# A graph attention layer on one core: the products of the segment sums dealt out among the pick products

## The chip, the cores and the metric

The kernel runs on one core of one Trainium2 chip. The metric is the time of one execution in microseconds (us) on the device. The time before is the median of three runs.

## What is computed

The layer has 6250 nodes of 64 values and 206250 edges, which come sorted by their destination. For each edge the scores of four heads are made of the source's key, the destination's query and the edge's own values; the score weighs the source's value, and the weighed values are summed by destination. Then comes a layer norm over the node.

```python
Qh = (x @ Wq.T + bq).reshape(n, H, D)          # n = 6250, H = 4, D = 16
Kh = (x @ Wk.T + bk).reshape(n, H, D)
Vh = (x @ Wv.T + bv).reshape(n, H, D)
Ee = (edge_attr @ We.T + be).reshape(-1, H, D)  # 206250 edges
score = (Kh[src] * Qh[dst] * (1.0 / np.sqrt(D)) * Ee).sum(-1)
score = jnp.exp(jnp.clip(score, -5.0, 5.0))
msg = Vh[src] * score[..., None]
wV = jax.ops.segment_sum(msg, dst, num_segments=n)
x = _layernorm(x + wV.reshape(n, H * D), axis=-1)
```

## The kernel before, in words

**Tiles, groups, steps.** The edges are cut into 1612 tiles of 128. Eight tiles are a group (202 groups, numbered g), and one turn of the main loop (L866 to L963) works on one group. Two groups are a step (numbered s; the last eight groups are steps of their own): the sums by destination are made once for a step. So the odd turn 2s+1 finishes a step's messages, and the even turn 2s+2 sums them.

**What each engine does in turn g, in the order of its own queue.** The order is written out by hand; the loop's text is the order of every engine's queue.

- TensorE (PE): `edges(g+3)` (2 fp32 products into `ee`), in some turns `picked_kv`, then `picks` (21 products of 128x512 in bf16 into one of two PSUM buffers `pick`), `turn(g+1)` (4 transposes of `term` into `qe`), `queries(g+2)` (2 products into `qq`), and in even turns `sums` (16 products of 128x192 in bf16 into `room`).
- VectorE (DVE): `products` (`prod`, `score`), `hots` (the one-hot rows `hot` that the next turn's picks read), `message` (`qe`), `take` twice, in odd turns `onehot_edges` (`of`, L723) and `add` (L804 and twice L810), then `terms(g+2)` (L707, which reads `qq` and `eb`) and parts of the layer norm.
- ScalarE (ACT): the exponential, `biased` (`eb`, out of `ee`), the one-hot rows for the queries (`to`), and `keep` twice (`msg`).
- GpSimd (POOL): indirect DMAs that gather keys and values by source (`kv`, L259), four steps ahead. SyncE (SP) issues the other loads, edges (`et`) and destination keys (`kb`) among them once in two turns.

**The picks.** For some tiles the keys and values are not gathered but picked by products with one-hot rows. `pieces(g)` gives a turn seven blocks, `by_two` deals them in pairs (2, 2, 2, 1), and each block is three products: the last of an even turn's four lots has three products, the others six. This goes on from turn 6 to turn 191.

**The sums.** `sums(s)` (L781) multiplies the step's one-hot columns `of` with the messages split into three bf16 parts, and adds over the 16 tiles in PSUM (`room`). Its first product needs three things of DVE: `of` of the step (made in turn 2s+1), the third parts of its messages (the second `take` of turns 2s and 2s+1), and that `add` of the step before has read `room`. That `add` stands in turn 2s+1 too, behind the second `take` and right ahead of `terms`. The messages' tiles of the first group are older.

**The gathers.** The list `where` collects marks, the PE product that was last issued at a place; the gathers of a turn are dealt evenly over the marks, and the first of each lot waits for its mark (`gather`, `behind`).

Of the kernel before, what the change touches and what calls it, by code (L numbers as in the profile page):

```python
# [21 lines left out]
G = 8  # L22
# [33 lines left out]
def tiles_in(s):  # L56
    return sum(tiles_of(g) for g in groups_of(s))


def groups_of(s):  # L60
    return range(STEPS[s][0], STEPS[s][0] + STEPS[s][1])
# [65 lines left out]
def tile_gnn(ctx: ExitStack, tc: tile.TileContext, x, x_blocks, by_rows, xT, wT, bias, beT, weT, eT, src, src_rows, dst,  # L127
# [159 lines left out]
    with tc.tile_pool(name="nodes", bufs=1) as nodes, \  # L287
# [27 lines left out]
        for i in range(NB // CB):  # L315
            s = slice(i * CB * P, (i + 1) * CB * P)
# [279 lines left out]
    with tc.If(rv == 0) as branch:  # L596

        with tc.tile_pool(name="work", bufs=2) as work, \
# [32 lines left out]
            def pieces(g):  # L631

                some, k, end = [], max(first_unit(g), 0), min(first_unit(g + 1), UNITS * LAST)
                while k < end:
                    some.append((k, min(end, k + MOST, (k // UNITS + 1) * UNITS)))
                    k = some[-1][1]
                return some
# [10 lines left out]
            def by_two(todo):  # L648

                blocks = [(k, w, w + 1 == end) for k, end in todo for w in range(k, end)]  # L650
                return [blocks[i:i + 2] for i in range(0, len(blocks), 2)]

            def picks(todo):

                for k, w, last in todo:
                    hot = HOT.pop(k) if last else HOT[k]
                    m, u = w // UNITS, w % UNITS
                    for part in range(3):
                        product(px[m % 2], parts[:, u, part].rearrange("p t c -> p (t c)"),
                                         hot[:, w - k, :], start=u == 0 and part == 0,  # L660
                                         stop=u == UNITS - 1 and part == 2)
# [20 lines left out]
            def product(*aps, **kw):  # L682
                mark.append(nc.tensor.matmul(*aps, **kw))  # L683
# [93 lines left out]
            def pa_of(s):  # L777

                return {NS - 3: px[0][:, :3 * C], NS - 2: px[1][:, :C], NS - 1: ee[:, 0, :C]}.get(s, pa)

            def sums(s):  # L781
                n = tiles_in(s)
                for j in range(n):
                    product(pa_of(s), (OF if s >= WHOLE else OH)[s][:, j, :],
                            MSG[s][:, j].rearrange("p i c -> p (i c)") if s < WHOLE else MSG[s][:, j, :],
                            start=j == 0, stop=j == n - 1,
                                     skip_group_check=True)
# [64 lines left out]
            ends = {groups_of(s)[-1]: s for s in range(NS)}  # L852
# [13 lines left out]
            for g in range(NG + 1):  # L866
                now, before = g < NG, g > 0
                todo, ahead = pieces(g), pieces(g + 1)
# [15 lines left out]
                parted = now and step_of[g] < WHOLE  # L884
# [27 lines left out]
                    picked_kv(READY.index(g - 2))  # L912
                    place_kv(READY.index(g - 2))
                where.append(mark[-1])
                for some in by_two(todo):
                    picks(some)
                    where.append(mark[-1])
                if g + 1 < NG:
                    turn(g + 1)
# [1 line left out]
                    queries(g + 2)  # L921
                where.append(mark[-1])
                if g - 1 in ends and now:
                    sums(ends[g - 1])
                if g + 4 < NG:
                    onehot_rows_rest(g + 4)
                if parted:
# [5 lines left out]
                for h in ([g] if g < NG - 3 else []) + ([g + 1] if NG - 4 <= g < NG - 1 else []):  # L933
                    if h not in ends:
                        continue
                    s = ends[h]
# [14 lines left out]
                if done:  # L951
# [8 lines left out]
                    for _ in range(3):  # L960
                        if normed < scaled:
                            norm(normed)
                            normed += 1  # L963
            sums(NS - 1)
            spreads(B - 2)
            assert normed == B - 2
# [9 lines left out]
    with branch.Else():  # L976

        sums = [dram.tile([NR, C], F32, name=f"sums{i}") for i in range(TABLES)]
# [108 lines left out]
        with tc.tile_pool(name="last", bufs=1) as last:  # L1087
            B = BIG + 1

            acc = last.tile([P, B, C], F32, name="gacc")  # L1090
            nc.sync.dma_start(acc, x_blocks)
            for i, s in enumerate(sums):
                part = last.tile([P, B, C], F32, name="part", bufs=2)
                (nc.sync, nc.scalar)[i % 2].dma_start(
                    part, s[:P * B, :].rearrange("(b p) c -> p b c", p=P))
                nc.vector.tensor_add(acc, acc, part)
            layer_norm(nc, last, acc, P, B)
            nc.sync.dma_start(out, acc)
# [43 lines left out]
```

## Time and profile before

| | |
|---|---|
| time, median of 3 runs | 2096.95 us (2089.41 to 2100.56) |
| the profiled execution's own time | 2094.31 us |
| its span, first to last instruction | 2092.5 us |
| mean granted TensorE clock | 0.889 of full |
| PE busy | 1697.4 us (81%), 7771 products |
| DVE busy | 1512.8 us (72%) |
| POOL busy | 1352.3 us (65%) |
| ACT busy | 899.7 us (43%) |
| DMA | 229.84 MB, mean 110 GB/s |

The rows of the profile's views name a line of the kernel, an engine, the operation and what it writes and reads (`room<-msg,of` writes the tile `room`). In a timeline a row has the start in us from the span's start, the duration in us, and behind the count, in brackets, the idle time of the engine before it and who ended it; "issue" is idle time for which the profile shows no one that was waited for. In a group's row stand the busy time in us and the mean duration of one in ns, then the idle time before its instructions. Durations of products overlap: the distance between two starts is what one costs.

### The profile page before, as it was taken

What the parts mean: (1) busy time and instruction counts of PE and PEld (TensorE: products, weight loads), DVE (VectorE), ACT (ScalarE), POOL (GpSimd) and SP (SyncE); (2) the same over time, 40 slices, a digit from 0 to 9 for tenths busy, and PEclk for the clock granted to TensorE, in tenths of its full rate; (3) what the DMA queues carried; (4) which work ended last, traced back from release to release, by engine and by line L of the source; (5) the groups of instructions that cost most, each with busy time, mean ns of one, the idle gap of its engine ahead of it and who ended that gap; (6) DMA issues with size and microseconds to landing.
All of it is one profiled execution on the core that took longest, in us unless ns stands there. A gap on an engine that the chain in (4) does not pass through costs nothing.

```text
span 2092.5 us, 24524 instructions
## 1 busy us (share of the span) xinstructions
PE 1697.4 (81%) x7771; PEld 843.7 (40%) x7771; DVE 1512.8 (72%) x2631; ACT 899.7 (43%) x1477; POOL 1352.3 (65%) x1414
## 2 busy tenths in 40 slices
PE   6538888888888888888888888888888898898874
PEld 6313444343444443444444344444343343444432
DVE  5347777777777677777777777767876776777876
ACT  3434444444444345444444444434444443444453
POOL 6666666666666666666666666666666666666643
PEclk9868999999899999998899899898998988988985
DMA  6733434343433443333334344343333433434431
GB/s 177 215 98 105 120 112 110 100 117 92 118 99 105 118 110 98 112 108 112 102 107 116 93 118 112 92 118 104 104 114 104 113 101 109 118 91 117 114 91 30
DMA packets 114977, 229.84 MB, mean 110 GB/s; under 512 B 55955, under 2 KB 56703, under 8 KB 114725
## 3 DMA queue, kind: packets, MB, share of 16 engines
q1 hardware_dynamic: 69474, 136.35, 21.6%
q0 software_dynamic: 44928, 90.79, 16.9%
q10 hardware_dynamic: 436, 1.04, 0.2%
q8 instruction: 63, 1.03, 0.2%
q14 instruction: 76, 0.62, 0.1%
HBM read 220.25 MB, written 7.82 MB: 109 GB/s over the span
## 4 chain that ended last, share of the span: by engine, by line
PE 60%; DVE 14%; issue 13%; ACT 5%; another core or an unknown queue 3%; DMA 3%; SPq 0%; DVEq 0%; POOL 0%; ACTq 0%; POOLq 0%
PE pick L683 40%; PE ee L683 8%; PE room L683 6%; PE qe L712 3%; PE qq L683 2%; DVE hot L643 2%; DMA qw<-q_tab 2%; DVE prod L731 2%; DVE score L734 2%; DVE qe L769 1%; ACT to L242 1%; DVE term L707 1%; ACT eb L694 1%; DVE msg L769 1%
## 5 line engine op out<-in xcount | busy, mean ns | idle before, releaser
L259 POOL DMA_INDIRECT kv<-kv_tab,src_i x1364 | 1312.8, 962 | 692.9 <-issue 320.9
L683 PE MATMUL pick<-hot,parts 128*128 128x512 bf16 x3900 | 976.9, 402 | 76.1 <-issue 68.4
L683 PEld LDWEIGHTS <-parts 128*128 128x128 bf16 x3900 | 396.1, 103 | 684.2 <-issue 331.6
L740 ACT ACTIVATE score<-score 128x32 f32<-128x32 f32 x202 | 46.3, 229 | 984.5 <-DVE score L736 654.9
L643 DVE TENSOR_TENSOR hot<-from,still 128x1024 bf16<-128x1024 bf16 (+4 forms) x379 | 394.2, 1043 | 0.0
L707 DVE TENSOR_TENSOR term<-eb,qq 128x512 f32<-128x512 f32 x202 | 137.7, 682 | 291.3 <-PE pick L683 147.5
L683 PE MATMUL ee<-et,we_sb 128*128 128x512 f32 x404 | 262.0, 728 | 53.3 <-issue 24.8
L683 PE MATMUL room<-msg,of 128*128 128x192 bf16 x1592 | 188.9, 266 | 122.0 <-issue 97.2
L764 ACT ACTIVATE msg<-qe 128x512 bf16<-128x512 f32 x400 | 237.2, 593 | 16.8 <-issue 6.6
L248 ACT ACTIVATE to<-to,one_p 126x1024 bf16<-126x1024 bf16 x198 | 226.4, 1143 | 0.0
L242 ACT ACTIVATE to<-kb,minus_row 126x1024 bf16<-126x1024 bf16 x198 | 224.6, 1135 | 0.0
L769 DVE TENSOR_TENSOR qe<-qe,msg 128x512 f32<-128x512 f32 x200 | 139.7, 699 | 117.4 <-ACT msg L764 81.8
L683 PEld LDWEIGHTS <-of 128*128 128x128 bf16 x1600 | 141.5, 105 | 162.7 <-issue 137.8
L769 DVE TENSOR_TENSOR msg<-qe,msg 128x512 bf16<-128x512 f32 x200 | 137.4, 687 | 86.8 <-issue 40.6
L694 ACT ACTIVATE eb<-ee,be_col 128x512 f32<-128x512 f32 x202 | 136.4, 675 | 109.6 <-PE pick L683 47.7
L712 PE MATMUL qe<-ident,term 128*128 128x128 f32 x806 | 131.5, 287 | 52.8 <-DVE term L707 44.6
L712 PEld LDWEIGHTS qe<-ident,term 128*128 128x128 f32 x806 | 104.7, 148 | 107.5 <-DVE term L707 57.1
L731 DVE TENSOR_TENSOR prod<-kv,qe 128x512 f32<-128x512 f32 x202 | 137.4, 680 | 12.1 <-remote 6.6
L734 DVE TENSOR_REDUCE score<-prod 128x32 f32<-128x512 f32 x202 | 138.3, 685 | 7.0
L752 DVE TENSOR_TENSOR qe<-kv,score 128x512 f32<-128x512 f32 x200 | 138.9, 695 | 4.3 <-ACT score L740 2.7
L723 DVE TENSOR_TENSOR of<-still,key 128x2048 bf16<-128x2048 bf16 (+2 forms) x105 | 123.0, 1173 | 0.2
L683 PEld LDWEIGHTS ee<-et,we_sb 128*128 128x128 f32 x404 | 71.8, 217 | 95.4 <-issue 54.7
(138 smaller groups left out, 848.5 us busy)
## 6 DMA issues: line engine op xcount, KB each, us to landing
et<-in_eT SPq DMA_DIRECT2D x100, 512.0 KB
kb<-key_tab SPq DMA_DIRECT2D x101, 504.0 KB
kv<-kv_tab,src_i POOLq DMA_INDIRECT x1364
srcs<-in_src_rows SPq DMA_DIRECT2D x52, 256.0 KB
qw<-q_tab SPq DMA_DIRECT2D x202, 15.8 KB
kv_tab<-kv_sb SPq DMA_DIRECT2D x4, 640.0 KB
q_tab<-q SPq DMA_DIRECT2D x5, 480.0 KB
y<-in_x_blocks SPq DMA_DIRECT2D x2, 512.0 KB
```

Of the source, the lines that this page charges most:

```text
L242: nc.scalar.activation(TO[g][:, :n, :], KB.pop(g)[:, :n * P].rearrange("p (j e) -> p j e", j=n), AF.Square, bias=minus_row3[:3 * W])
L248: nc.scalar.activation(TO[g][:, :n, :], TO[g][:, :n, :], AF.Relu, bias=one_p[:3 * W], scale=-1.0)
L259: return nc.gpsimd.indirect_dma_start(out=kv_of(g)[:, j, :], out_offset=None, in_=kv_tab[:, :], in_offset=bass.IndirectOffsetOnAxis(ap=src ...
L643: nc.vector.tensor_tensor(HOT[k][:, :hi - lo].rearrange("p b (a c) -> p b a c", c=2), pairs(FROM[m])[:, None].to_broadcast(shape), block2[ ...
L683: mark.append(nc.tensor.matmul(*aps, **kw))
L694: nc.scalar.activation(EB[g][:, :n], ee[:, :n], AF.Identity, bias=be_col)
L707: nc.vector.tensor_mul(TERM[g][:, :n], EB.pop(g)[:, :n], qq[:, :n])
L712: nc.tensor.transpose(qe[g % 2][:, 2 * u:2 * u + 2, :].rearrange("p j c -> p (j c)"), TERM[g][:, u, :], ident)
L731: nc.vector.tensor_mul(prod[:, :n, :], kv_of(g)[:, :n, :C], qe[g % 2][:, :n, :])
L734: nc.vector.tensor_reduce(score, prod[:, :n, :].rearrange("p g (h d) -> p g h d", h=H), axis=AX.X, op=OP.add)
L764: nc.scalar.activation(part, left, AF.Copy)
L769: nc.vector.tensor_sub(left if i == 0 else part_of(g, 2)[1], left, part)
```

## The change

`sums` gets a range of tiles. In an even turn with picks, four of its products are issued behind the second, the third and the fourth lot of picks, twelve in all. The last four stay where all sixteen stood, behind the transposes and the queries. Where a turn has no picks (the first and the last ones), and for the last two steps, nothing is moved. The marks in `where` are taken behind the dealt-out products. No instruction is added and none is taken away.

```diff
-            def sums(s):
+            def sums(s, lo=0, hi=2 * G):
                 n = tiles_in(s)
-                for j in range(n):
+                for j in range(lo, min(hi, n)):
                     product(pa_of(s), (OF if s >= WHOLE else OH)[s][:, j, :],
                             MSG[s][:, j].rearrange("p i c -> p (i c)") if s < WHOLE else MSG[s][:, j, :],
                             start=j == 0, stop=j == n - 1,
...
-                for some in by_two(todo):
+                summed = 0
+                for i, some in enumerate(by_two(todo)):
                     picks(some)
+                    if i and parted and g - 1 in ends:
+                        sums(ends[g - 1], summed, summed + 4)
+                        summed += 4
                     where.append(mark[-1])
                 if g + 1 < NG:
                     turn(g + 1)
@@
                 where.append(mark[-1])
                 if g - 1 in ends and now:
-                    sums(ends[g - 1])
+                    sums(ends[g - 1], summed)
```

## The prediction

> **What bounds the kernel now.** I read the page first: its busy line, its chain, and its costliest groups.
>
> ```profile
> PE 1697.4 (81%) x7771; PEld 843.7 (40%) x7771; DVE 1512.8 (72%) x2631; ACT 899.7 (43%) x1477; POOL 1352.3 (65%) x1414
> ...
> PE 60%; DVE 14%; issue 13%; ACT 5%; another core or an unknown queue 3%; DMA 3%; SPq 0%; DVEq 0%; POOL 0%; ACTq 0%; POOLq 0%
> ...
> L683 PE MATMUL pick<-hot,parts 128*128 128x512 bf16 x3900 | 976.9, 402 | 76.1 <-issue 68.4
> ...
> L707 DVE TENSOR_TENSOR term<-eb,qq 128x512 f32<-128x512 f32 x202 | 137.7, 682 | 291.3 <-PE pick L683 147.5
> ...
> L683 PE MATMUL room<-msg,of 128*128 128x192 bf16 x1592 | 188.9, 266 | 122.0 <-issue 97.2
> ```
>
> PE carries 60% of the chain and DVE 14%: PE is the bound, and DVE has a little slack, which shows in its idle time ahead of `term`, 291.3 us in 202 (1.44 us each), most of it behind PE. The row to look at is the last one. The sums are a fifth of PE's products but have the most idle time of all, 122.0 us, and 97.2 us of it has no releaser. The timeline of PE shows what that is; the first seven rows are an even turn and what follows it, the others a later even turn and its odd one.
>
> ```profile
> 604.54 0.92 PE L683 MATMUL room<-msg,of 128*128 128x192 bf16 x9
> 605.91 0.32 PE L683 MATMUL room<-msg,of 128*128 128x192 bf16 x2 [0.45 <-issue]
> 607.33 0.33 PE L683 MATMUL room<-msg,of 128*128 128x192 bf16 x2 [1.09 <-issue]
> ...
> 609.48 0.32 PE L683 MATMUL room<-msg,of 128*128 128x192 bf16 x1 [0.46 <-issue]
> 610.19 1.87 PE L683 MATMUL ee<-et,we_sb 128*128 128x512 f32 x2 [0.39 <-issue]
> 611.85 5.17 PE L683 MATMUL pick<-hot,parts 128*128 128x512 bf16 x21
> 616.85 0.60 PE L712 MATMUL qe<-ident,term 128*128 128x128 f32 x4
> ...
> 645.35 1.49 PE L683 MATMUL room<-msg,of 128*128 128x192 bf16 x16
> ...
> 653.81 0.59 PE L683 MATMUL pick<-hot,parts 128*128 128x512 bf16 x2 [1.02 <-issue]
> 655.24 0.38 PE L683 MATMUL pick<-hot,parts 128*128 128x512 bf16 x1 [0.84 <-issue]
> 655.95 0.38 PE L683 MATMUL pick<-hot,parts 128*128 128x512 bf16 x1 [0.34 <-issue]
> 656.67 0.38 PE L683 MATMUL pick<-hot,parts 128*128 128x512 bf16 x1 [0.33 <-issue]
> 656.88 0.60 PE L712 MATMUL qe<-ident,term 128*128 128x128 f32 x4
> ```
>
> Undisturbed, a run of sixteen starts its last product 1.25 us after its first (1.49 less the 0.24 of one product): 0.083 us each. In a slow stretch PE gets one product in about 0.7 us (605.91 to 607.33 is two, 655.24 to 655.95 one), whether it is a sum or a pick. So the run of sixteen is often slow, but where it isn't, the picks behind it are: the stretch comes once in two turns and hits what stands there. From the first sum to the next transposes the first pair of turns took 616.85 - 604.54 = 12.31 us, the second 656.88 - 645.35 = 11.53 us.
>
> **The change part by part.** The count of PE's instructions stays, and no buffer changes. There are 92 even turns with picks between 175 and 1994 us, of which the terms below are counted (one more is in the start).
>
> (a) *Order on PE.* Twelve sums of 0.083 us, 1.0 us, now run ahead of the transposes and the queries, and 1.0 us less behind them. A turn's work is the same: 0.
>
> The next rows are PE's in turns 8, 28 and 188, and DVE's second `add` row (`below`) in each, which ends last of what the first sum needs.
>
> ```profile
> 176.86 4.70 PE L683 MATMUL pick<-hot,parts 128*128 128x512 bf16 x21
> ...
> 377.72 4.70 PE L683 MATMUL pick<-hot,parts 128*128 128x512 bf16 x21
> 383.43 0.66 PE L712 MATMUL qe<-ident,term 128*128 128x128 f32 x4 [1.01 <-DVE term L707]
> ...
> 1980.36 4.70 PE L683 MATMUL pick<-hot,parts 128*128 128x512 bf16 x21
> ```
> ```profile
> 180.16 0.28 DVE L810 SCALAR_TENSOR_TENSOR acc<-room,below,acc 128x64 f32<-128x64 f32 x1
> ...
> 382.50 0.28 DVE L810 SCALAR_TENSOR_TENSOR acc<-room,below,acc 128x64 f32<-128x64 f32 x1
> ...
> 1983.78 0.28 DVE L810 SCALAR_TENSOR_TENSOR y<-room,below,y 128x64 f32<-128x64 f32 x1
> ```
>
> (b) *The new place to wait.* The first sum needs DVE's `add` of the turn before. It stood behind 21 picks, 4 transposes and 2 queries; now it stands behind 12 picks. Behind it in PE's queue are 9 picks, the transposes and the queries, and for these DVE's `term`, and the picks' `hot` buffers. What a pick costs is in the row at 377.72 us: 4.70 us for 21, less 0.38 for the last, over 20: 0.216.
>
> In turn 28 twelve picks are done at 377.72 + 2.59 = 380.31 us and the `add` at 382.78: PE would stand 2.47 us. It stands 1.01 there now, at the transposes. Read in this way over all 92 turns, 22 have the `add` late; the first is turn 8 (179.45 against 180.44, 0.99 us) and the last turn 188 (1982.95 against 1984.06, 1.11 us). They come to 19.6 us, of which about 2.8 us are waits that stand at the transposes already: 17 us. In the other 70 the `add` is done before the twelfth pick, and the wait costs nothing.
>
> (c) *DVE later.* The queries of an even turn end 1.0 us later, and DVE's `term` waits for them; with it everything that DVE does up to the next `add` can come 1.0 us later while PE's twelfth pick does not. If all of it came through, 36 turns would be late, by 46 us, less 3. If nothing did (DVE behind anyway, or held by ACT), 17 us stand. The row of `term` has about half its idle time behind picks and the rest elsewhere, so I take half: 30 us.
>
> (d) *Waits that coincide.* In 16 of the 22 late turns the run of sums is slow as well (its last start over 1.5 us after its first). What supplies PE can go on while PE waits for DVE, so part of these waits, 12.5 us of the 19.6, may only take the place of a slow stretch. The bounds are 0 and 12.5; I take half, -6: 24 us are left.
>
> (e) *The slow stretch meets other instructions.* In a slot of 0.7 us a sum does 0.083 us of work and a pick 0.216, so a stretch on picks loses 0.133 us less of each slot, 19%. If all 97.2 us moved from sums to picks, that gives 18 us; if it stayed on sums, 0; if the stretch went away, 12.31 - 11.53 = 0.78 us for each of the 50 slow runs of the 92, 39 us. Four sums still stand behind the queries and four right ahead of the transposes, where the stretch begins now. I take half of the middle case: -9.
>
> ```profile
> L731 DVE TENSOR_TENSOR prod<-kv,qe 128x512 f32<-128x512 f32 x202 | 137.4, 680 | 12.1 <-remote 6.6 <-issue 3.6 <-DMA kv<-kv_tab,src_i 0.2
> ```
> ```profile
> SPq L203 <- PE pick L683: 608.6, 36, 25.8
> ```
> ```profile
> PE pick L683 <- DVE x L665: 20.4, 16, 2.0
> ```
>
> (f) *Things that ride along.* The gathers behind the third to last mark are released 0.3 to 1.0 us later. POOL runs four steps ahead, and `prod` waited 0.2 us for gathered `kv` in the whole span; cost 0, and if that cover went, up to the 1.0 us of a turn. SP's load of `et` waits for PE's first products of an even turn, ahead of everything moved, and in part for picks (36 times), which come at most 0.67 us later; it loads six groups ahead: 0. Where an even turn ends a batch of picks, its last pick comes 0.67 us later and DVE's next step with it; PE waits for that step now 20.4 us in all, in 16 turns. Cost between 0 and 26 batches by 0.67, 17 us; 0, since that step of DVE stands behind a whole turn's other work.
>
> *Sum:* 30 - 6 - 9 = +15 us. On the profiled execution's 2094.31 us (span 2092.5) that is 2109; on the median of the runs, 2.6 us above it, 2112. I forecast **2110 us**.
>
> **The clock.** The next rows follow turn 28: PE's timeline, and busy times by stretch with the mean granted clock as the third number from the right.
>
> ```profile
> 389.51 0.37 PE L683 MATMUL pick<-bkv_p,ones_b 3*128 3x512 bf16 x1 [2.04 <-DVE x L665]
> 389.81 1.16 PE L683 MATMUL pick<-w,x 128*128 128x128 f32 x8
> 390.80 6.38 PE L683 MATMUL pick<-hot,parts 128*128 128x512 bf16 x21
> ```
> ```profile
> 383.40:388.00 4.60, 3.54 (x24) 2.18 (x25) 4.40 (x8) 2.36 (x5) 3.38 (x5) 1.00 0.33 86
> ...
> 390.80:397.00 6.20, 6.20 (x23) 2.53 (x21) 4.17 (x7) 2.41 (x5) 3.00 (x4) 0.72 0.13 36
> ```
>
> A wait can also cost clock. In turn 29 PE waited 2.04 us for DVE, and the picks behind it ran partly at half clock. The 21 picks took 6.38 us instead of 4.70, 1.68 us more, at a mean granted clock of 0.72, while the wait of 1.01 us at 383.43 left the clock at 1.00. The Trainium skill, page "TensorE: Matmul & The Clock Gate", section "Why this matters for your kernels", asks for no gaps over about 3 us between bursts of products; by that rule none of the new waits, 2.47 us at most, would cost clock. The rows differ: 2.04 us with work around it that was thin was enough.
>
> **The rivals.**
>
> *Forecast, the wait decides (0.45).* Terms as above. For it: the `add` is the last thing in DVE's odd turn, and 22 waits can be read off. Against it: 70 turns have it early, by up to 5 us.
>
> *The run of sixteen was what made the stretch (0.24, faster).* Sums ask for instructions at more than twice the rate of picks (0.083 against 0.216 us). If the supply only fails when a dense row of short instructions stands behind the transposes, dealing them out ends it at this place, from the point on where the four that are left no longer run it dry. The price is (e)'s end, -39 us, and with (b) to (d), +24, the sum is -15: 2079 us; if the waits fall into slow stretches as well, 2060. For it: the slow rows at 605.91 begin behind the ninth sum of such a row. Against it: in the second pair the same stretch hits plain picks.
>
> *It comes out even (0.26).* The waits lie in slow stretches (all of (d)) and the stretch moves on to picks (all of (e)'s middle): 30 - 12.5 - 18 = 0, 2094 to 2097 us.
>
> *The waits cost clock too (0.05, slower).* If each of the 22 waits took 1.68 us, 37 us on top: 2146. Against it: only one of them is over 2 us as the trace stands, and five with the 1.0 us of (c).
>
> **How the numbers follow.** About 0.5%, 10.5 us, is what can be told from no change here. The forecast's own bounds are (b) without (c) and with all of (d) and (e), 17 - 12 - 18 = -13, to 43 us without (d) and (e). So slower holds 0.46, most of the forecast's share and the clock's; within 0.5% holds 0.29, the even case and a part of the forecast's; faster 0.25. The range goes from 2070, below the faster rival's 2079, to 2140, the forecast's upper bound; what it leaves out is the faster rival's far end and the clock.
>
> **What would show it.** (b): behind the twelfth pick, sums that wait for DVE's `add` (L810), in 20 to 36 turns, 20 to 45 us in all, where the group of the sums shows next to none in the loop now; the wait of the transposes for `term` in even turns smaller. (c): more idle time of DVE ahead of `term` in even turns. (e): idle time without a releaser ahead of the sums clearly below 97.2 us, and that of the picks (68.4) and of `ee` above what they have. If the sums' falls and the picks' doesn't rise, the faster rival holds. If the sums wait for DVE in under ten turns, (b) is wrong. If the granted clock falls below 0.87, the last rival holds.

## The result, and the profile after

The changed kernel takes 2093.43 us (median of 20 runs, 2089.87 to 2099.18), the kernel before beside it 2094.67 us (20 runs). The ratio is 0.9994, 95% interval 0.9985 to 1.0003: no change. On another chip it was 1.0000 (0.9991 to 1.0009). The forecast was 2110 us.

The rows of the changed kernel's page that answer to those of before (groups: busy us, mean ns of one, idle time before them, what ended it):

```profile
PE 1685.2 (81%) x7771; PEld 842.9 (40%) x7771; DVE 1514.9 (72%) x2631; ACT 899.1 (43%) x1477; POOL 1354.2 (65%) x1414
...
PE 57%; DVE 18%; issue 14%; ACT 5%; another core or an unknown queue 3%; DMA 2%; POOL 1%; DVEq 0%; SPq 0%; ACTq 0%; POOLq 0%
...
L259 POOL DMA_INDIRECT kv<-kv_tab,src_i x1364 | 1314.6, 964 | 688.6 <-issue 328.8
L683 PE MATMUL pick<-hot,parts 128*128 128x512 bf16 x3900 | 978.6, 397 | 37.6 <-issue 35.1
...
L707 DVE TENSOR_TENSOR term<-eb,qq 128x512 f32<-128x512 f32 x202 | 138.0, 683 | 352.1 <-PE room L683 122.3
L683 PE MATMUL room<-msg,of 128*128 128x192 bf16 x1592 | 223.9, 262 | 108.3 <-issue 69.5
```

The sums' idle time without a releaser fell from 97.2 to 69.5 us and the picks' from 68.4 to 35.1. But PE's idle time as a whole is 2092.0 - 1685.2 = 406.8 us, where it was 2092.5 - 1697.4 = 395.1: what left these two rows went elsewhere. The view of PE's waits says where. Its columns are us in all, times, and the longest; first the kernel before, then the changed one, both from turn 8 to turn 191, so that the start and the end of the program stay out.

```profile
PE room L683 <- issue: 97.2, 108, 2.6
PE pick L683 <- issue: 89.1, 147, 2.0
PE ee L683 <- issue: 24.3, 31, 1.9
...
PE qe L712 <- DVE term L707: 10.7, 6, 4.2
PE qq L683 <- issue: 8.8, 7, 1.8
PE qe L712 <- issue: 6.0, 10, 1.1
```
```profile
PE room L683 <- issue: 69.5, 82, 2.6
PE qe L712 <- issue: 60.4, 64, 2.7
PE pick L683 <- issue: 53.0, 99, 2.0
...
PE ee L683 <- issue: 12.9, 17, 1.4
PE qq L683 <- issue: 11.6, 14, 2.4
...
PE qe L712 <- DVE term L707: 6.0, 5, 2.4
PE room L683 <- DVE y L810: 5.7, 7, 1.7
PE room L683 <- DVE room L804: 5.3, 4, 1.7
```

The five rows "issue" come to 97.2 + 89.1 + 24.3 + 8.8 + 6.0 = 225.4 us before and 69.5 + 60.4 + 53.0 + 12.9 + 11.6 = 207.4 after. That is about the same: two kernels below that have no waits of this kind and take the same time, `behind_picks` and `add_early_before`, have 205.6 and 229.5 us in these rows. What changed is its place. It has moved on in the queue to the transposes, 6.0 to 60.4 us, which now follow the first twelve sums directly. The transposes' wait for `term` shrank by 10.7 - 6.0 = 4.7 us, and the sums got waits on DVE that they did not have. Turn 28 in PE's timeline shows such a wait; it stands where the prediction put it:

```profile
374.68 2.75 PE L683 MATMUL pick<-hot,parts 128*128 128x512 bf16 x12
378.81 0.49 PE L683 MATMUL room<-msg,of 128*128 128x192 bf16 x4 [1.37 <-DVE acc L810]
379.13 1.46 PE L683 MATMUL pick<-hot,parts 128*128 128x512 bf16 x6
...
381.74 0.60 PE L712 MATMUL qe<-ident,term 128*128 128x128 f32 x4
```

A wait is read here as the time from the start of the pick ahead of the first sum to the start of that sum, less the 0.216 us of a pick. Over the loop 25 turns have one of over 0.1 us, 23.8 us in all, 1.82 us the longest. Counted from the first `ee` product of a turn to that of the next (turns 8 to 187), even turns became longer, 10.47 to 11.31 us, and odd turns shorter, 9.57 to 8.76; a pair stays at 20.04 and 20.07 us.

### The profile page after: what moved, and what is told of

It reads as the page before. It is cut to its first block, busy times and chain, and to the rows that moved or that the text cites. A ratio compares the mean times of both kernels' runs of the same rounds, so it can differ in the third digit from the quotient of the medians.

```text
span 2092.0 us, 24524 instructions
## 1 busy us (share of the span) xinstructions
PE 1685.2 (81%) x7771; PEld 842.9 (40%) x7771; DVE 1514.9 (72%) x2631; ACT 899.1 (43%) x1477; POOL 1354.2 (65%) x1414
## 4 chain that ended last, share of the span: by engine, by line
PE 57%; DVE 18%; issue 14%; ACT 5%; another core or an unknown queue 3%; DMA 2%; POOL 1%; DVEq 0%; SPq 0%; ACTq 0%; POOLq 0%
PE pick L683 36%; PE ee L683 8%; PE room L683 6%; PE qe L712 3%; DVE hot L643 3%; PE qq L683 2%; DVE score L734 2%; DVE prod L731 2%; DVE qe L769 2%; DVE of L723 2%; ACT to L242 1%; DVE msg L769 1%; DVE qe L752 1%; ACT msg L764 1%
## 5 line engine op out<-in xcount | busy, mean ns | idle before, releaser
L259 POOL DMA_INDIRECT kv<-kv_tab,src_i x1364 | 1314.6, 964 | 688.6 <-issue 328.8
L683 PE MATMUL pick<-hot,parts 128*128 128x512 bf16 x3900 | 978.6, 397 | 37.6 <-issue 35.1
L683 PEld LDWEIGHTS <-parts 128*128 128x128 bf16 x3900 | 395.1, 103 | 574.9 <-issue 248.6
L707 DVE TENSOR_TENSOR term<-eb,qq 128x512 f32<-128x512 f32 x202 | 138.0, 683 | 352.1 <-PE room L683 122.3
L683 PE MATMUL room<-msg,of 128*128 128x192 bf16 x1592 | 223.9, 262 | 108.3 <-issue 69.5
L683 PEld LDWEIGHTS <-of 128*128 128x128 bf16 x1600 | 146.3, 103 | 216.1 <-issue 128.9
L712 PE MATMUL qe<-ident,term 128*128 128x128 f32 x806 | 144.4, 295 | 105.9 <-issue 73.5
L769 DVE TENSOR_TENSOR msg<-qe,msg 128x512 bf16<-128x512 f32 x200 | 137.4, 687 | 91.0 <-ACT msg L764 42.0
L769 DVE TENSOR_TENSOR qe<-qe,msg 128x512 f32<-128x512 f32 x200 | 139.7, 698 | 52.1 <-ACT msg L764 37.3
```

What stands on the lines that cost most here:

```text
L259: return nc.gpsimd.indirect_dma_start(out=kv_of(g)[:, j, :], out_offset=None, in_=kv_tab[:, :], in_offset=bass.IndirectOffsetOnAxis(ap=src ...
L712: nc.tensor.transpose(qe[g % 2][:, 2 * u:2 * u + 2, :].rearrange("p j c -> p (j c)"), TERM[g][:, u, :], ident)
L769: nc.vector.tensor_sub(left if i == 0 else part_of(g, 2)[1], left, part)
```

## The experiments

Two theories. **B**: the waits cost their 24 us, and the slow stretch gave about 24 us back; two terms that happen to cancel. **C**: PE doesn't hold the loop; something else does, and PE's waits, whatever ends them, take slack that is there anyway. (**A**, between them: a wait is absorbed by the slow stretch of its own pair of turns.)

One plain fact is needed to read the numbers. The runs fell on chips of two kinds: on the first the kernel before takes 2095 to 2121 us, on the second 1796 to 1797 us. Every run in the table stands beside runs of the kernel before on its own chip, and its ratio is to these.

| kernel | us | before there | ratio, 95% interval |
|---|---|---|---|
| sums_first | 2101.43 | 2094.74 | 1.0032 (1.0017 to 1.0047) |
| behind_picks | 2094.84 | 2094.74 | 1.0002 (0.9990 to 1.0014) |
| add_early_after | 2093.27 | 2094.74 | 0.9993 (0.9978 to 1.0007) |
| add_early_before | 2095.74 | 2094.74 | 0.9995 (0.9980 to 1.0009) |
| half_sums | 2088.16 | 2095.96 | 0.9958 (0.9943 to 0.9972) |
| two_parts | 2085.35 | 2095.96 | 0.9956 (0.9939 to 0.9973) |
| no_loads | 2093.75 | 2095.96 | 0.9993 (0.9980 to 1.0006) |
| no_gathers | 1727.90 | 2095.96 | 0.8244 (0.8213 to 0.8275) |
| no_marks | 1797.24 | 1796.96 | 1.0002 (0.9992 to 1.0012) |
| half_gathers (the kernel before again) | 1797.50 | 1796.96 | 1.0007 (0.9996 to 1.0017) |
| no_gathers_after | 1673.25 | 1796.96 | 0.9316 (0.9300 to 0.9331) |
| no_gathers_sums_first | 1681.39 | 1796.96 | 0.9367 (0.9351 to 0.9383) |
| changed_again | 2118.67 | 2119.44 | 1.0000 (0.9991 to 1.0009) |
| half_gathers_true | 1740.13 | 2119.44 | 0.8211 (0.8192 to 0.8231) |
| plain_loads | 1739.47 | 2119.44 | 0.8208 (0.8191 to 0.8226) |
| no_gathers_again | 1731.41 | 2119.44 | 0.8170 (0.8151 to 0.8189) |
| no_marks_again | 1797.08 | 1795.64 | 1.0008 (0.9998 to 1.0018) |
| changed_no_marks | 2402.53 | 2121.16 | 1.1331 (1.1316 to 1.1347) |

### Other places for the sums: many waits, little time

`sums_first` puts all sixteen sums ahead of the picks of an even turn, where their waits on DVE are the longest that can be had; `behind_picks` puts the run of sixteen behind the last lot of picks.

```diff
+                early_sums = todo and parted and g - 1 in ends
+                if early_sums:
+                    sums(ends[g - 1])
                 for some in by_two(todo):
                     picks(some)
...
-                if g - 1 in ends and now:
+                if g - 1 in ends and now and not early_sums:
                     sums(ends[g - 1])
```

> All sixteen sums stand ahead of the picks of the even turn. In the trace of before DVE's add ends 1.4 us behind the first pick's start on the mean of 92 even turns, after it in 75 of them, 144 us in all (253 us if DVE comes 1.33 us later as well). If the waits and the slow stretch are two terms that cancelled (B): at least 100 us slower than before, 5%. If waits are absorbed by the slow stretch of the same pair of turns (A): much less than the wait that the trace shows, under half of it, 20 to 70 us. If the loop is not bound by PE at all (C): same as before.

> All sixteen sums stand undealt behind the 21 picks and ahead of the transposes of the even turn. DVE's add is late there in 1 of 92 turns, under 1 us in all, so it has next to none of the wait and none of the dealing. B: slow stretches as before, time within 0.3% of before. The run of sixteen as the cause: still a run, still slow, same as before. A: same as before.

The sums of `sums_first` in the groups with their releasers:

```profile
L683 PE MATMUL room<-msg,of 128*128 128x192 bf16 x1592 | 187.1, 282 | 135.7 <-DVE y L810 63.9 <-DVE room L804 40.9 <-DVE acc L810 15.0
```

63.9 + 40.9 + 15.0 = 119.8 us of waits on the `add`, 101.2 of them between turns 8 and 191, where the kernel before has none; and the time went up by 6.7 us. At this price, 6.7 / 101.2 = 0.07 us for a us of wait (0.04 to 0.10 by the interval), the changed kernel's 23.8 us would cost 1.6 us. That is C's (or A's) answer; B needs the full price. A has a part in it: the rows "issue" of these five products fell from 225.4 to 164.7 us over these turns, well below the 205.6 of `behind_picks`, so some 61 us of the waits took the place of the slow stretch. `behind_picks` neither deals nor waits, and comes out the same too.

### The add made earlier

In the changed kernel the `add` moves ahead of the batch's `picked` in every turn, so that the sums find it done; the same edit in the order of before is the control.

```diff
-                if g > groups_of(ONES - 1)[-1]:
-                    for s in done:
-                        add(s)
+                for s in done:
+                    add(s)
...
-                if g <= groups_of(ONES - 1)[-1]:
-                    for s in done:
-                        add(s)
```

> The changed kernel, with DVE's add moved up in its odd turn to ahead of onehot_edges and the second take, so that the first sum waits for the second take, 0.95 us earlier. The 25 waits of 23.8 us in the trace after become about 12 of 6 us. B: 15 to 18 us faster than the changed kernel, 0.8%. A or C: within 0.3% of it.

> The kernel before with the same early add, as the control: the wait behind the queries was never there, so all theories say within 0.3% of before, unless DVE now waits for PE's sums.

From turn 8 to turn 191 the sums of `add_early_after` don't wait for the `add` at all (idle times of over 0.15 us), where the changed kernel has 5.7, 5.3 and 1.4 us (`y`, L804, `acc`) in twelve waits; 7.6 us on `of` came up. The waits of the change are mostly gone, and the time did not follow: 0.9993, against 0.9994 with them.

### Taking work away

`half_sums` and `two_parts` take products out of PE, `no_loads` the repeated loads out of SP's queue, `no_gathers` the gathers out of POOL.

```diff
-                for j in range(n):
+                few = s < WHOLE and s > 2
+                for j in range(0, n, 2 if few else 1):
...
-                            start=j == 0, stop=j == n - 1,
+                            start=j == 0, stop=j == n - (2 if few else 1),
```
```diff
-                    for part in range(3):
+                    for part in range(0, 3, 2):
```
```diff
-        et = loads.tile([P, LG * G // 2, P], F32, name="et")
-        nc.sync.dma_start(et[:, :hi - lo, :], eT[:, lo:hi, :])
+        if q < 4:
+            kept_et.append(loads.tile([P, LG * G // 2, P], F32, name="et"))
+            nc.sync.dma_start(kept_et[q][:, :hi - lo, :], eT[:, lo:hi, :])
+        et = kept_et[q % 4]
```
```diff
         (g, js), after = lot
+        if 20 <= g < NG - 12:
+            return
         for j in js:
```

(In `no_loads` the load of `kb` is kept in the same way, for its first four tiles.)

> The kernel before, with every second product of the sums left out (776 of 1612; the sums then miss half of the edges). PE bound by its work: 776 by 0.083 us, 64 us less at most. PE bound by the number of its instructions (the supply, 10% of its instructions gone): 100 to 200 us less. PE not the bound of the loop: within 0.5% of before.

> The kernel before, with the middle one of the three products of each pick block left out (1300 of 3900; the picked keys and values lose bits). By PE's work: 1300 by 0.216 us, 281 us less. By the number of instructions, 17% of PE's: 200 to 300 us less. PE not the bound: within 1% of before. What the time falls by less than 281 us is what others hold.

> The kernel before without the loads of et and kb from turn 2 on, so that it works on the edges and keys of the first turns again and again. If the slow stretch of PE is tied to these 1 MB bursts: idle time of PE without a releaser under 60 us instead of some 220 us. If PE is the bound: 200 to 400 us faster. If the bound is elsewhere (DVE with ACT, or POOL): the stretch goes and the time hardly moves, under 3%.

> The kernel before without the gathers of groups 20 to 189, which then use old keys and values. POOL issues a gather every 1.25 us, 13.7 in a pair of turns, 17.1 us of 20.0. If POOL, or the traffic of its gathers, holds the loop: 10% faster or more. If not: within 1%, or as much faster as the slow stretch shrinks.

The picks in the groups of `two_parts`, and then the chain and the picks of `no_gathers`:

```profile
L683 PE MATMUL pick<-hot,parts 128*128 128x512 bf16 x2600 | 719.5, 426 | 113.5 <-issue 109.4
```
```profile
DVE 62%; ACT 20%; PE 9%; issue 5%; another core or an unknown queue 2%; DMA 1%; POOL 1%; POOLq 0%; DVEq 0%; SPq 0%; ACTq 0%
...
L685 PE MATMUL pick<-hot,parts 128*128 128x512 bf16 x3900 | 900.1, 387 | 5.9 <-issue 5.5
```

1300 picks less are 1300 x 0.216 = 281 us of PE's work, and the run is 10.6 us shorter; the picks that are left stand 109.4 us idle without a releaser instead of 68.4, and the mean granted clock went down from 0.889 to 0.830. PE's work is not the bound. Without loads nothing changes. Without gathers 368 us go, with every product in place, the slow stretch goes with them (5.5 us), and the chain passes to DVE. It is the gathers that hold this loop.

### The order, where no gather holds the loop

The same gathers are left out of the changed order and of `sums_first`. These ran on the second kind of chip, `no_gathers` and `no_gathers_again` on the first.

> The changed order (sums four at a time behind the pairs of pick blocks), with the gathers of the loop left out from group 20 up to the last 12, to be set against the same with the order of before, which took 0.824 of before's time (1727.9 us). Theory C: without the gathers the loop is bound by VectorE (87% busy) and TensorE (89%) and the order counts: the waits of the first sum on VectorE's add, 24 us in the changed kernel, now cost, so 1735 to 1755 us, ratio 0.828 to 0.838. Rival, theory B (the waits and the slow stretch are two terms of about 24 us that cancel): the slow stretch is gone without gathers, so that only the waits are left: the same 1750 us. Rival, theory A (waits are absorbed by what is slow in the same pair of turns anyway): with nothing slow, the same 24 us. If it is equal within 0.3%, the order never mattered, with or without gathers.

> All sixteen sums ahead of the picks in even turns, which cost 0.3% (6.7 us) with the gathers in place although the sums waited some 120 us on VectorE, with the gathers of the loop left out as before. Theory C (what the gathers impose is slack in which TensorE's waits vanish): without them the waits cost most of their length, 60 to 120 us, so 1790 to 1850 us, ratio 0.855 to 0.88. If the order never matters because VectorE leads and TensorE follows with slack of its own: within 10 us of 1728, ratio 0.823 to 0.829.

> The order of before without the gathers of groups 20 to the last 12, to stand on one chip with the changed order without them (0.9316 of before on the chip where before is 1797 us). If these runs are on that kind of chip: theory C says the same within 0.3% when VectorE's chain bounds (64% of the chain of the changed one): ratio 0.929 to 0.934; theories A and B, whose waits of 24 us have no slow stretch to vanish in, say that it is shorter: 0.915 to 0.922. On the other kind of chip: 0.8244 again.

> The changed kernel itself, unaltered, beside the runs below. The last four kernels ran on a chip on which the kernel before takes 1797 us instead of 2095 and TensorE shows no idle time without a releaser (0 us ahead of the pick products and of the sums instead of 68 and 97), with the gathers in place: it has the waits without the slow stretch. If these runs are on such a chip: theory B (waits of 24 us and a gain of 24 us in the slow stretch cancel) leaves only the waits, 1815 to 1825 us, ratio 1.010 to 1.016. Theory C (what else holds the loop gives TensorE slack, so that its order doesn't count): within 0.3%, ratio 0.997 to 1.003, with the same 20 to 30 us of waits ahead of the sums and as much less idle time elsewhere. On a chip like the first ones: the ratio of the first comparison, 0.9985 to 1.0003, again.

The total times can't be set against one another across chips: the start before the loop differs between them. DVE's timeline has the loop by itself. `prod` is DVE's first step of a turn; these rows are turns 24 and 180, in `no_gathers`, then in `no_gathers_after`:

```profile
311.75 0.65 DVE L733 TENSOR_TENSOR prod<-kv,qe 128x512 f32<-128x512 f32 x1
...
1544.95 0.68 DVE L733 TENSOR_TENSOR prod<-kv,qe 128x512 f32<-128x512 f32 x1
```
```profile
265.74 0.66 DVE L733 TENSOR_TENSOR prod<-kv,qe 128x512 f32<-128x512 f32 x1
...
1500.38 0.68 DVE L733 TENSOR_TENSOR prod<-kv,qe 128x512 f32<-128x512 f32 x1
```

1544.95 - 311.75 = 1233.20 us in the order of before, 1500.38 - 265.74 = 1234.64 in the changed one, for 78 pairs of turns: 1.4 us, 0.1%. With all the sums first it is 1234.9 us. In these stretches of the loop the sums wait on DVE for the following times (us and times), first in `no_gathers_after`, then in `no_gathers_sums_first`; in `no_gathers` they have no such wait:

```profile
  DVE y L812: 7.8, 16
  DVE acc L812: 0.6, 1
```
```profile
  DVE y L812: 62.0, 50
  DVE acc L812: 2.2, 2
```

So here are 8.4 us of waits in the changed order, with no slow stretch that could give anything back, and the loop is 1.4 us longer; with 64.2 us of waits it is 1.7 us longer. **B falls**, by the second figure above all. A isn't needed here: the waits cost next to nothing where the stretch that should absorb them is absent. What I expected for C in the first of these texts was wrong too: I thought that with the gathers gone the order would count. It doesn't, because DVE (62% and 64% of the chain) then sets the pace, and PE, although 89 and 91% busy, catches up. One thing isn't separated: order and kind of chip differ together in this comparison. `no_gathers_sums_first` shares its chip with `no_gathers_after` and shows that the order costs nothing there; `no_gathers_again` gave 1233.3 us on a second chip of the first kind. `changed_again` fell on the first kind of chip too and so only repeats the first comparison.

### What it is in the gathers

> The order of before, with every second gather of the loop left out from group 20 up to the last 12 (part of the rows of kv is then not fetched). Some 590 of 1364 gathers go. If each gather costs the loop its pitch (theory C, a straight line between before at 2095 us and all gathers left out at 1728 us), this run takes some 1910 us, ratio 0.91. If the gathers bind only where they are closer than the other engines' work (GpSimd as a pacer that has slack when halved), it is at the floor of the run without gathers, 1730 to 1760 us, ratio 0.83 to 0.84. TensorE's idle time ahead of the pick products without a releaser falls from 68 us to about half in the first case, to under 10 in the second.

This kernel was a slip: its lots hold one gather each, so that "every second of a lot" left none out. It is the kernel before once more, and gives its profile on the second kind of chip:

```profile
PE 30%; DVE 29%; DMA 19%; ACT 9%; issue 8%; POOL 4%; DVEq 0%; SPq 0%; POOLq 0%; ACTq 0%
...
L259 POOL DMA_INDIRECT kv<-kv_tab,src_i x1364 | 1313.2, 963 | 415.9 <-issue 186.4
L685 PE MATMUL pick<-hot,parts 128*128 128x512 bf16 x3900 | 910.6, 391 | 0.0
```

There the slow stretch is absent with all gathers in place (0.0 us ahead of the picks). POOL gathers every (1313.2 + 415.9) / 1364 = 1.27 us, on the first kind every (1314.6 + 688.6) / 1364 = 1.47 us.

The gathers cost time on this kind of chip as well, but in another way, which can be seen in DVE's waits:

```profile
DVE prod L733 <- DMA kv<-kv_tab,src_i: 95.7, 52, 4.6
```

Here `prod` waits for gathered rows, where it waited 0.2 us on the first kind. From turn 24 to turn 180 the loop takes 1338.7 us here, 1562.3 us in the kernel before on the first kind, and 1234.6 without gathers (`no_gathers_after`, on this chip). So gathers cost some 104 us on this kind of chip: a pair of turns takes 1338.7 / 78 = 17.2 us here, as long as its 13.7 gathers at 1.25 us each. Another 224 us come on the first kind, where PE's idle time without a releaser is 194.0 us in those turns; here it is 0.

The next two take out every second gather, and replace all of them by plain loads of the same size by SP.

```diff
         for j in js:
+            if 20 <= g < NG - 12 and j % 2:
+                continue
             ins = gather_kv(g, j)
```
```diff
         for j in js:
-            ins = gather_kv(g, j)
+            if 20 <= g < NG - 12:
+                lo = (g * G + j) % 32 * P
+                ins = nc.sync.dma_start(kv_of(g)[:, j, :], kv_tab[lo:lo + P, :])
+            else:
+                ins = gather_kv(g, j)
```

> The kernel of before with every second gather of the loop (odd tiles of a group) left out from group 20 to the last 12; the kernel labelled half_gathers left none out, since its lots hold one gather each and the slice kept that one, so it was the kernel before once more. If each gather costs the loop a share of its own (theory C on a chip with the slow stretch): half way between before and the run with none, ratio 0.90 to 0.92 where before is 2095 us. If the gathers bind only where GpSimd's pitch of 1.25 us is the longest chain: the time of the run without gathers, ratio 0.83 there, or 0.93 to 0.94 where before is 1797 us, with TensorE's idle time without a releaser gone.

> The kernel of before with the gathers of groups 20 to the last 12 replaced by plain loads of as many rows and bytes (128 rows of 512 B that lie together), issued by SyncE: the same landings and bytes, but no descriptors made by GpSimd and no picking of rows by index. Theory C with the landings as the cost (a gather's 16 queues signalling semaphores, or its bytes): on a chip with the slow stretch it stays near before, ratio 0.95 to 1.0, with 60 us and more of idle time without a releaser ahead of the pick products. With GpSimd's own work as the cost: the time of the run without gathers, ratio 0.82 to 0.85, idle time under 10 us. On a chip without the stretch: 0.93 to 0.95 either way, since GpSimd's pitch is gone, and it decides nothing.

Leaving out half the gathers is nearly as good as leaving out all (0.8211 against 0.8170 on one chip), and plain loads in place of the gathers cost no more (0.8208). It is neither the bytes nor a fixed price for each gather; what is left is that gathers stand close together. The plain loads differ from gathers in two things, who issues them and that their rows lie together; which of the two counts isn't separated. The last three drop the mark that the first gather of a lot waits for:

```diff
             ins = gather_kv(g, j)
-            if j == js[0]:
-                behind(ins, after)
```

> The order of before; the gathers of GpSimd no longer wait for a matmul of TensorE (the dependence that ties the first gather of each lot to a place in TensorE's order is dropped), only for their rows and their buffers. Theory C (the gathers hold the loop by their own pitch: 17 of them a pair of turns, 1.25 us each when nothing is waited for, 21 us by the mean pitch of 1.457 less what marks hold back): GpSimd's waits on PE of some 230 us go, and if these waits are what lengthens its pitch the run is 1 to 3% shorter, 2030 to 2075 us. Rival, theory C2 (the marks cost nothing since GpSimd follows and doesn't lead; the gathers hold the loop by slowing the other engines while they run): the same time within 0.5%, with gathers that stand in bunches and, inside a bunch, TensorE's idle time without a releaser.

> The order of before without the gathers' waits on matmuls, once more: on the chip where before is 1797 us it changed nothing (1.0002), but GpSimd hardly waited there (mean pitch 1.269 us). On the other chips, where before is 2095 to 2119 us and GpSimd's mean pitch is 1.47 to 1.49 with 230 us of waits on TensorE: if these waits hold the loop (TensorE late, so gathers late, so the rest late) the run falls to 1800 to 1900 us, ratio 0.86 to 0.90. If dense gathers themselves slow TensorE, whatever starts them, it stays within 1% of before, ratio 0.99 to 1.01, with TensorE's idle time without a releaser still above 60 us ahead of the pick products and GpSimd held by its buffers instead. On a chip where before is 1797 us: 1.000 again.

> The changed order and no waits of the gathers on matmuls, in one kernel, since the two kinds of chips answer one question each. Where before takes 1797 us, leaving the waits out gave 1.0002 and 1.0008 in the order of before, so what is left is the changed order, with all gathers and without TensorE's slow stretch: theory B (waits of 24 us whose cancelling gain is missing there) 1.010 to 1.016; theory C (GpSimd's pitch and VectorE hold the loop, TensorE's order has slack) 0.997 to 1.003. Where before takes 2095 to 2119 us, the changed order gave 0.9994 and 1.0000, so what is left is the waits of the gathers: if GpSimd's waits on TensorE hold the loop, 0.86 to 0.90; if dense gathers slow TensorE whatever starts them, 0.99 to 1.01, with over 60 us of idle time without a releaser ahead of the pick and sum products.

`no_marks` was twice on the second kind of chip and changed nothing there. `changed_no_marks` was on the first kind, and is 13.3% slower; the changed order with its marks was at 0.9994 and 1.0000 there, so it is the marks. Neither of my two cases for it was right, since both let the marks cost time or do nothing: on this kind of chip they save 280 us, by spacing the gathers. The timeline of POOL and that of PE over the same 20 us of this kernel:

```profile
1205.68 0.94 POOL L259 DMA_INDIRECT kv<-kv_tab,src_i  x1 [0.99 <-DVE qe L750]
1206.92 0.94 POOL L259 DMA_INDIRECT kv<-kv_tab,src_i  x1 [0.30 <-issue]
...
1214.41 0.94 POOL L259 DMA_INDIRECT kv<-kv_tab,src_i  x1 [0.30 <-issue]
1220.59 0.94 POOL L259 DMA_INDIRECT kv<-kv_tab,src_i  x1 [5.24 <-DVE qe L750]
```
```profile
1207.15 2.61 PE L681 MATMUL pick<-hot,parts 128*128 128x512 bf16 x10
1210.37 1.02 PE L681 MATMUL pick<-hot,parts 128*128 128x512 bf16 x4 [0.61 <-issue]
1211.80 1.10 PE L681 MATMUL pick<-hot,parts 128*128 128x512 bf16 x4 [0.41 <-issue]
1213.93 0.59 PE L681 MATMUL pick<-hot,parts 128*128 128x512 bf16 x2 [1.03 <-issue]
1216.84 1.11 PE L710 MATMUL qe<-ident,term 128*128 128x128 f32 x4 [2.33 <-issue]
...
1224.90 1.46 PE L681 MATMUL pick<-hot,parts 128*128 128x512 bf16 x6
```

Eight gathers run 1.25 us apart from 1205.68 on. PE's stalls begin in the middle of them and grow to 2.33 us; none follows in the 5.24 us for which POOL pauses, and six picks take 1.46 us again at 1224.90. One place is not a proof, so I counted the picks that stand directly behind a pick (turns 20 to 190), by the gathers that began in the 6 us ahead of the earlier of the two. In this kernel, of 814 picks with at most two such gathers three came more than 0.55 us behind the pick before; of 1061 with five, 91. In the kernel before it is 11 of 705 with three gathers and 56 of 1088 with five, in the changed one 2 of 579 and 31 of 1102. In `no_marks` on the second kind of chip, of 2527 with five, none. So the slow stretch is what dense gathers do to PE on the first kind of chip. Both kernels issue the same gathers at nearly the same pitch, so both have the same stretch, in whatever products happen to be due.

The Trainium skill, page "Perfetto Trace Analysis", section "DMA Instruction — SWDGE (GPSIMD)", says that the end which the profiler shows for such an instruction is the writing of its last descriptor, not the end of its transfer. The traces fit that without showing it: a gather's row is 0.963 us on the second kind of chip and 0.964 on the first, while the loop differs by 14%. POOL's rows alone don't show this cost.

## Why the prediction was wrong

**"PE carries 60% of the chain and DVE 14%: PE is the bound."** This is the step that failed, and most of the rest follows from it. The chain named the engine on which time was spent, but 13% of it was "issue" and the last row that I pointed to, the sums' 97.2 us without a releaser, said that PE had been held by something that the profile doesn't name. An engine so held isn't the bound. The check that I lacked was to ask what a us of PE's work is worth: 281 us of picks taken out gave 10.6 us, 0.04 for one.

**(a)** The order on PE costs nothing by itself: right (`behind_picks` 1.0002).

**(b) and (c), the new place to wait:** the mechanism and the size were right. The text gave 20 to 36 turns and 20 to 45 us, 17 us of it without (c) and 30 with half of (c); 25 turns and 23.8 us came, from turn 8 (0.91 us, forecast 0.99 without (c)) to turn 188 (0.40, forecast 1.11). DVE's idle time ahead of `term` rose as (c) said, 291.3 to 352.1 us. The transposes' wait for `term` shrank by 4.7 us in the loop, forecast 2.8. What was wrong is that these us were taken to put off the end: +30 in the sum, 24 less what was spared in the trace, and nothing in the time. They were worth 0.07 us each in `sums_first`, and without gathers 1.7 / 64.2 = 0.03.

**(d), waits that coincide with slow stretches, -6:** the mechanism was near the truth, too narrow in its kind. Waits do take the place of the slow stretch (some 61 of 101 us in `sums_first`), but not only those in sixteen turns: nearly all waits cost nothing. And as they cost nothing without a slow stretch either, the coincidence alone doesn't make them free: PE has time left over in a pair of turns.

**(e), the slow stretch meets other instructions, -9:** it did move, as said, but not on to picks and `ee`, whose idle time without a releaser fell (68.4 to 35.1 and 24.8 to 12.9 us), but to the transposes. Its length, 225.4 and 207.4 us, stayed within what kernels of the same time have (205.6 to 229.5), so that no gain from it can be told.

**(f)** Nothing rode along: the gathers' pitch is the same, 1.47 us. But "cost 0, `prod` waited 0.2 us for gathered `kv`" overlooked what gathers cost without anyone's waiting for them.

**The rivals.** *The run of sixteen made the stretch* fell: the stretch lies over other products in the changed kernel and goes with the gathers alone. Its sign came true all the same (the sums' idle time fell, the picks' didn't rise), since I had not thought of the transposes as the place where the stretch could go. *It comes out even* came next to the time, with 2094 to 2097 us, but by luck: 30 - 12.5 - 18 lets two real terms cancel, which is B, and that isn't the account shown. *The waits cost clock too* fell: the mean clock is 0.894, and the longest of the new waits 1.82 us. The rule of the Trainium skill that the prediction names (page "TensorE: Matmul & The Clock Gate", section "Why this matters for your kernels"), no gaps over about 3 us, gave the right answer for the mean, but the trace doesn't bear it out as enough. The clock records of the changed kernel change at multiples of 3.41 us; of 526 such windows between 200 and 2000 us 91 were followed by half clock, and the longest wait of PE in any of these is 2.65 us.

**What stays open:** by which path dense gathers keep PE from its next instruction on the first kind of chip. It isn't PE alone: DVE's `msg` (L769) stands 40.6 us idle without a releaser in the kernel before, in 71 waits, and never on the second kind. Semaphores from DVE to ACT aren't late there: ACT's `exp` starts 34 ns behind DVE's clip in the median, in both kernels and on both kinds of chip. Loads and bytes don't do it. And the changed order hasn't been run on the second kind of chip with all its gathers.

None of the kernels that compute the whole beats either of the two by more than its interval. What the runs point to is fewer or wider spaced gathers; the 18% that half of them were worth on the first kind of chip is a bound, since the rows left out have to be had in some other way. More rows picked instead of gathered would be one, which wasn't tried.

## What to carry to other kernels

Before you price a wait on the engine with the longest chain, find out what a us of that engine's work is worth: take a large piece of its work out and see whether the time follows. Idle time that nothing in the profile releases is a sign that the engine is being held from outside, and a new wait may then only take the place of a part of it. A transfer for which nobody waits can still hold the loop, by what it does to the others while it is issued; whether it does is shown by leaving half of it out.

## What the runs showed of the hardware

- Chips differ in what dense gathers cost. The same kernel takes 1796 to 1797 us on two chips and 2095 to 2121 us on others, with a gather's row at 963 and 962 ns and DVE's `hot` at 1043 ns on both. From turn 24 to turn 180 the difference is 224 us, and PE's idle time without a releaser is 194.0 us there on the one kind and 0 on the other. It comes with gathers close together: in the kernel before, 1.6% of the picks are over 0.55 us behind the pick before them where three gathers began in 6 us, and 5.1% where five did.
- Waits that look like a cost can save time: the gathers' waits for marks in PE's order save 280 us of 2402 on a chip of the first kind (in the changed order), and nothing on the second (in the order of before).
- A freed PE runs at a lower clock: with a third of the picks left out the mean granted clock fell from 0.889 to 0.830, with half of the sums left out to 0.864. With the gathers left out and all products in place it rose to 0.942.
